# Edge scores of two graph attention layers as products of two rows per graph, in strips of the TensorE array

## The chip, the cores and the metric

The kernel runs on one core of a Trainium2 chip. Its time is the device time of one execution in microseconds (us), the median of several runs.

The kernel treats 128 graphs in 32 groups of four, and in the steady part every group takes the same time. In the trace I take the distance from the first `pw` matmul of one group to that of the next, and call the median the **period**.

## The reference

Two layers on `x` [128 graphs, 128 nodes, 256] with an adjacency matrix for each graph. The first is a relational attention with eight heads and a feed-forward network (FFN). The second, which the change touches, has two graph attention layers, then a norm, an FFN and another norm:

```
def _gat(h, adj, W, a, out_features):
    Wh  = h @ W
    Wh1 = Wh @ a[:out_features]          # one number per node
    Wh2 = Wh @ a[out_features:]          # one number per node
    e = leaky_relu(Wh1 + swapaxes(Wh2, 1, 2), 0.2)     # 128 x 128 edge scores
    att = softmax(where(adj > 0, e, -9e15), axis=1)
    return att @ Wh
h = _gat(x, adj, W1, a1); h = _gat(h, adj, W2, a2)
h = layernorm(residual + h); out = layernorm(h + ffn(h))
```

The edge scores of a graph are an outer sum of two vectors.

## The kernel before

All matmuls are fp32. The order of TensorE is written by hand: `beside(main, side)` puts units of an FFN between the pieces of the graph layers, and a `yield n` in a piece means "n FFN units here". A unit is two `ph` matmuls of 128x512 with one ScalarE activation (`hT`), or four `po` matmuls of 128x256; either occupies TensorE for about 1.72 us. The matmuls write to eight buffers in the memory called PSUM: four `ps_s`, two `ps_av` ("av" and "den"), two `ps_mm` for the FFN.

The outer sum was made of a broadcast and a bias. `pb` has the one vector in all 128 rows (a matmul whose stationary operand is one column repeated 128 times), and ScalarE adds the other vector as a bias for each partition:

```
def edges(pb, bias, S, l):
    for b in range(G):                                          # G = 4 graphs
        nc.scalar.activation(s[:, b, :], pb[:, b*P:(b+1)*P], AF.Identity, bias=bias(b))
    nc.vector.scalar_tensor_tensor(s, s, ALPHA, s, op0=ALU.mult, op1=ALU.max)   # leaky relu
    nc.scalar.activation(s, s, AF.Exp)
    ...                                  # mask, row sums, reciprocal; POOL multiplies

def layer1(S, after):
    ...
    yield 4
    yT = transposed(...)                       # pt -> yT
    yield 1
    for b in range(G):                         # pw -> wh, in ps_s
        ...
    pb = ps_av.tile([P, T], F32, tag="den")
    for c in range(NCH):                       # NCH = 2, T = 512
        nc.tensor.matmul(pb, wb[:, c, :], yT[:, c, :], ...)
    att = edges(pb, lambda b: wh[:, b, D+2:D+3], S, 0)
    after()                                    # transposes of the next group: pt, in ps_s
    yield 5
    for b in range(G):
        nc.tensor.matmul(py[:, :D+1], att[:, b, :], wh[:, b, :D+1], ...)
        nc.scalar.copy(yh[:, b, :], py[:, :D+1])
        nc.tensor.matmul(pb[:, b*P:(b+1)*P], wh[:, b, D+1:D+2].to_broadcast([P, P]), att[:, b, :], ...)
    att = edges(pb, lambda b: yh[:, b, D:D+1], S, 1)
    yield 5
    ...                                        # pg: att @ yh
```

## Time and profile before

| quantity | before |
|---|---|
| time, median | 3167.5 us |
| period of a group | 95.48 us |
| TensorE busy | 95% of the span |
| TensorE waits for `hT`, second FFN (beside the graph layers) | 25.9 us in all |
| TensorE waits for `hT`, first FFN | 34.3 us in all |

The page and the timelines that carry the argument are shown in the prediction. One view more: the list of who waited for whom, TensorE's part (us in total, times, the longest). Three lines are shown; those left out come once or twice each, the largest a wait of 37.1 us for weights at the start.

```profile
PE ph L279 <- ACT hT L283: 60.2, 60, 1.1
PE pt L259 <- DVE t L242: 16.1, 5, 6.5
PE py L466 <- POOL gs L436: 6.5, 1, 6.5
```

Only the first line recurs in each group: twice, once in the FFN beside the graph layers and once in the other FFN. The other two belong to the ends of the kernel, where there is no FFN to fill the time.

### The profile page before, as it was taken

The page shows a single profiled execution, that of the slowest core. Times are in us where ns is not written, and L with a number is a line of the kernel's source. Part 1 is how long each engine was busy: PE and PEld are TensorE (multiplying, and loading weights), DVE is VectorE, ACT ScalarE, POOL GpSimd, SP SyncE. Part 2 cuts the span into 40 slices and gives each one's busy share as a digit, 9 for nine tenths or more (in the row PEclk, how much of TensorE's full clock was granted, in tenths as well). Part 3 has the DMA queues.
Part 4 walks back from the last instruction along what each step waited for, and adds up shares of the span by engine and source line. Part 5 has one row for each costly group of instructions (what it writes and reads, how often), then busy time and mean ns, then how long its engine had stood idle before and what let it go on. Part 6 is the DMA issues. An engine that isn't in the chain of part 4 may idle for free.

```text
span 3165.2 us, 42834 instructions
## 1 busy us (share of the span) xinstructions
PE 3015.7 (95%) x18062; PEld 2016.9 (64%) x18062; DVE 1636.4 (52%) x3433; ACT 1139.4 (36%) x1958; POOL 747.4 (24%) x360
## 2 busy tenths in 40 slices
PE   4899999999999999999999999999999999999997
PEld 2556667666666666666666666666666666676664
DVE  3544465554465554565554555544555644555622
ACT  1333333434333334333334333334333334334332
POOL 0212221212222212222212222212212212212222
PEclk9999999999999999999999999999999999999998
DMA  4000000000000000000000000000000000000000
GB/s 148 21 17 17 24 18 17 21 24 18 18 23 18 21 24 18 17 18 24 21 18 24 17 17 21 24 18 24 17 17 21 24 18 24 18 17 8 8 7 14
DMA packets 58101, 69.80 MB, mean 22 GB/s; under 512 B 6704, under 2 KB 44720, under 8 KB 57904
## 3 DMA queue, kind: packets, MB, share of 16 engines
q1 hardware_dynamic: 51632, 64.76, 6.7%
q10 hardware_dynamic: 6272, 2.25, 0.4%
q8 instruction: 144, 2.36, 0.3%
q14 instruction: 53, 0.43, 0.0%
HBM read 50.22 MB, written 16.78 MB: 21 GB/s over the span
## 4 chain that ended last, share of the span: by engine, by line
PE 88%; ACT 9%; DVE 1%; DMA 1%; issue 0%; POOL 0%; ACTq 0%; SPq 0%; POOLq 0%; DVEq 0%
PE po L290 28%; PE ph L279 23%; PE pv L391 7%; PE pq L381 5%; PE pav L351 4%; PE pw L451 4%; PE pwo L411 3%; PE ps L318 2%; PE pt L259 2%; PE pden L341 2%; PE py L466 2%; PE pg L481 2%; PE pb L458 2%; ACT yT L262 1%; ACT L426 1%; ACT L238 1%
## 5 line engine op out<-in xcount | busy, mean ns | idle before, releaser
L279 PE MATMUL ph<-yT,w_L_gnn_W 128*128 128x512 f32 x1024 | 484.9, 597 | 34.3 <-ACT hT L283 34.3
L279 PE MATMUL ph<-yT,w_L_gnn_w_ff 128*128 128x512 f32 x1024 | 464.5, 597 | 25.9 <-ACT hT L283 25.9
L249 POOL TENSOR_TENSOR res<-t,r_L_gnn_g 128x1024 f32<-128x1024 f32 x64 | 150.7, 2355 | 1375.4 <-DVE rs L240 1335.6
L290 PE MATMUL po<-w_L_gnn_W,hT 128*128 128x256 f32 x2048 | 472.1, 384 | 0.0
L290 PE MATMUL po<-w_L_gnn_w_ff,hT 128*128 128x256 f32 x2048 | 457.5, 379 | 0.0
L242 DVE TENSOR_SCALAR t<-t,mv,rs 128x256 f32<-128x256 f32 x384 | 447.6, 1226 | 3.5
L290 PEld LDWEIGHTS po<-w_L_gnn_w_ff,hT 128*128 128x128 f32 x2048 | 386.5, 190 | 65.3 <-issue 14.8
L290 PEld LDWEIGHTS po<-w_L_gnn_W,hT 128*128 128x128 f32 x2048 | 381.4, 190 | 62.2 <-issue 6.6
L279 PEld LDWEIGHTS ph<-yT,w_L_gnn_W 128*128 128x128 f32 x1024 | 192.8, 191 | 290.2 <-issue 223.4
L395 DVE TENSOR_TENSOR v<-pv,r_L_gnn_bv 128x512 f32<-128x512 f32 x128 | 88.6, 692 | 489.5 <-PE pv L391 489.5
L279 PEld LDWEIGHTS ph<-yT,w_L_gnn_w_ff 128*128 128x128 f32 x1024 | 187.8, 191 | 239.6 <-issue 178.7
L283 ACT ACTIVATE hT<-ph,c_L_gnn_b 128x512 f32<-128x512 f32 x256 | 175.9, 688 | 452.7 <-PE ph L279 452.4
L249 POOL TENSOR_TENSOR res<-t,r_L_gnn_g_ln 128x1024 f32<-128x1024 f32 x64 | 150.4, 2350 | 453.2 <-DVE rs L240 388.7
L391 PE MATMUL pv<-wv,xT 128*128 128x512 f32 x512 | 240.2, 592 | 0.0
L283 ACT ACTIVATE hT<-ph,c_L_gnn_b_ff 128x512 f32<-128x512 f32 x256 | 171.7, 682 | 162.5 <-PE ph L279 162.5
L358 DVE RECIPROCAL rd<-pden 128x512 f32<-128x512 f32 x64 | 214.3, 3349 | 20.4 <-PE pden L341 20.3
L326 DVE TENSOR_TENSOR pm<-e,adj 128x512 f32<-128x512 f32 x256 | 159.5, 684 | 114.7 <-ACT e L325 114.7
L238 ACT ACTIVATE sd<-mv,eps 128x4 f32<-128x4 f32 x96 | 28.1, 292 | 501.1 <-DVE mv L236 501.1
L235 DVE BATCH_NORM_STATS2 st<-t 128x6 f32<-128x256 f32 x512 | 192.7, 413 | 6.6
L325 ACT ACTIVATE e<-ps 128x512 f32<-128x512 f32 x256 | 132.2, 602 | 151.6 <-PE ps L318 151.3
L436 POOL TENSOR_TENSOR gs<-gs,gr 128x512 f32<-128x512 f32 x64 | 66.6, 1041 | 496.9 <-DVE gr L435 484.8
L391 PEld LDWEIGHTS pv<-wv,xT 128*128 128x128 f32 x512 | 94.9, 190 | 108.1 <-issue 108.1
(101 smaller groups left out, 3705.9 us busy)
## 6 DMA issues: line engine op xcount, KB each, us to landing
xT<-in_xT_dram SPq DMA_DIRECT2D x32, 512.0 KB, 3.7
x<-in_x_dram SPq DMA_DIRECT2D x32, 512.0 KB, 3.9
out_dram<-res SPq DMA_DIRECT2D x32, 512.0 KB, 2.9
adj<-in_adjT_dram SPq DMA_DIRECT2D x32, 256.0 KB, 2.7
w_L_gnn_W<-in_L_gnn_W_dram SPq DMA_DIRECT2D x2, 1024.0 KB, 8.2
w_L_gnn_w_ff<-in_L_gnn_w_ff_dram SPq DMA_DIRECT2D x2, 1024.0 KB, 12.1
wv<-in_L_gnn_Wv_dram SPq DMA_DIRECT2D x2, 256.0 KB, 7.0
temp<-in_L_gnn_a_dram ACTq DMA_DIRECT2D x2, 256.0 KB, 9.8
```

The costliest lines, as they stand in the source:

```text
L235: nc.vector.bn_stats(st[:, b, :], t[:, b, :])
L242: nc.vector.tensor_scalar(t[:, b, :], t[:, b, :], mv[:, b, 0:1], rs[:, b : b + 1], op0=ALU.subtract, op1=ALU.mult,)
L249: nc.gpsimd.tensor_mul(o, y, over(gr))
L279: nc.tensor.matmul(ph, wa[:, c, f * P : (f + 1) * P], inT[:, c, :], start=(c == 0), stop=(c == NCH - 1),)
L283: nc.scalar.activation(hT[:, f, :], ph, func, bias=ba[:, f : f + 1])
L290: nc.tensor.matmul(po[:, s * D : (s + 1) * D], hT[:, f, b * P : (b + 1) * P], wb_[:, f, :], start=(f == 0), stop=(f == NF - 1),)
L325: nc.scalar.activation(e[:, s], pss[s], AF.Exp, scale=SCALE)
L326: nc.vector.tensor_mul(pm[:, s], e[:, s], ad[:, 2 * p : 2 * p + 2, None, :].to_broadcast([P, 2, NCH, P]),)
L351: nc.tensor.matmul(pav[s * DH : (s + 1) * DH, u, c, :], v[:, d0 : d0 + DH], m[:, s, u, c, :], start=(r == 0), stop=(r == 1),)
L358: nc.vector.reciprocal(rd, pden)
L381: nc.tensor.matmul(pq, w[:, c, m * P : (m + 1) * P], xt[:, c, :], start=(c == 0), stop=(c == NCH - 1),)
L391: nc.tensor.matmul(pv, xt[:, c, b * P : (b + 1) * P], wv[:, c].rearrange("p r d -> p (r d)"), start=(c == 0), stop=(c == NCH - 1),)
```

## The change

The intent is to make TensorE's part cheaper. An outer sum is a product of two pairs of rows: (u, 1) against (1, v). `ends` makes the two rows of each graph as matmuls with 32 stationary columns, one graph in each 32-column strip of the array. `edges` multiplies them as matmuls over 32 rows, one graph in each 32-row strip. Four such matmuls are meant to run side by side. The diff is abridged.

```diff
+    def ends(lhs, rhs, n):
+        pr = ps_av.tile([P, P], F32, tag="den", name="pr_" + n)
+        for c in range(len(lhs)):
+            for b in range(G):
+                nc.tensor.matmul(pr[b * DH : (b + 1) * DH, :], lhs[c](b), rhs[c](b), ...)
+        src = ...; tgt = ...
+        nc.vector.tensor_scalar(src, pr, rows01[:, 1:2], rows01[:, 0:1], op0=ALU.mult, op1=ALU.add)
+        nc.scalar.activation(tgt, pr, AF.Identity, bias=rows01[:, 1:2], scale=rows01[:, 0:1])
+        return src, tgt
-    def edges(pb, bias, S, l):
+    def edges(src, tgt, S, l):
-        for b in range(G):
-            nc.scalar.activation(s[:, b, :], pb[:, b*P:(b+1)*P], AF.Identity, bias=bias(b))
-        nc.vector.scalar_tensor_tensor(s, s, ALPHA, s, op0=ALU.mult, op1=ALU.max)
+        pes = [ps_s.tile([P, T], F32, tag="s", ...) for b in range(G)]
+        for b in range(G):
+            rows = slice(b * DH, (b + 1) * DH)
+            nc.tensor.matmul(pes[b][:, :P], src[rows, :], tgt[rows, :], start=True, stop=True)
+        for b in range(G):
+            pe = pes[b][:, :P]
+            nc.scalar.activation(s[:, b, :], pe, AF.Copy, scale=ALPHA)
+            nc.vector.tensor_max(s[:, b, :], pe, s[:, b, :])
...
         yield 1
+        both = ends(..., n + "_0")                # ahead of pw
...                                                # pw -> wh
-        pb = ...; matmul(pb, wb, yT)
-        att = edges(pb, ..., S, 0)
+        yield 1
+        att = edges(*both, S, 0)
         after()
-        yield 5
+        yield 4
+        both = ends([lambda b: wh[:, b, :DH]], [lambda b: att[:, b, :]], n + "_1")
...                                                # py; the second pb is gone
-        att = edges(pb, ..., S, 1)
-        yield 5
+        yield 1
+        att = edges(*both, S, 1)
+        yield 4
```

The weights prepared at the start change to match (`wr` in place of `wb`, two columns fewer beside the products). The number of FFN units stays the same; one of each five moves ahead of `edges`.

More of the change, by code (lines that the diff above doesn't have):

```diff
@@ L174, in mm_tile @@
         return ps_mm.tile([P, T], F32, tag="mm", name=name)
-    NU = D + 3
+    NU = D + 2
     temp = flat(w1p.tile([P, NF, T], F32, tag="hT", name="temp"))
@@ L193, in fast_pass @@
     wa2 = k.columns(gw2, a2, scr, "2")
-    rhs = cut(NCH, D + 2)
-    nc.vector.tensor_copy(rhs[:, :, :D], gw2)
-    nc.vector.tensor_copy(rhs[:, :, D : D + 1], wa2[:, :, 1:2])
-    nc.vector.tensor_copy(rhs[:, :, D + 1 : D + 2], wa2[:, :, 0:1])
+    rhs = cut(NCH, NU)
+    nc.vector.tensor_copy(rhs[:, :, :2], wa2)
+    nc.vector.tensor_copy(rhs[:, :, 2:], gw2)
     gw1T = cut(NCH, D)
@@ L206, in fast_pass @@
     wu = k.tile([P, NCH, NU], "wu")
-    wb = k.tile([P, NCH, P], "wb")
+    wr = k.tile([P, NCH, DH], "wr")
+    nc.vector.memset(wr, 0.0)
+    nc.vector.tensor_copy(wr[:, :, :2], wa1)
     for m in range(NCH):
@@ L211, in fast_pass @@
             nc.tensor.matmul(
-                pu[:, : D + 2], gw1T[:, c, m * P : (m + 1) * P], rhs[:, c, :],
+                pu[:, :NU], gw1T[:, c, m * P : (m + 1) * P], rhs[:, c, :],
                 start=(c == 0), stop=(c == NCH - 1),
             )
-        nc.scalar.copy(wu[:, m, : D + 2], pu[:, : D + 2])
-        nc.vector.tensor_copy(wu[:, m, D + 2 :], wa1[:, m, 1:2])
-        nc.vector.tensor_copy(wb[:, m, :], wa1[:, m, 0:1].to_broadcast([P, P]))
+        nc.scalar.copy(wu[:, m, :], pu[:, :NU])
+    rows01 = k.tile([P, 2], "rows01")
+    strips = k.ident.rearrange("p (s r) -> p r s", r=DH)
+    nc.vector.tensor_reduce(rows01, strips[:, 0:2, :], AX.X, ALU.add)
     c_adj = k.tile([P, NG], "c_adj")
@@ L415, in layer0 @@
             added(t, p, po, xr)
-    def edges(pb, bias, S, l):
+    def ends(lhs, rhs, n):
+        pr = ps_av.tile([P, P], F32, tag="den", name="pr_" + n)
+        for c in range(len(lhs)):
+            for b in range(G):
+                nc.tensor.matmul(
+                    pr[b * DH : (b + 1) * DH, :], lhs[c](b), rhs[c](b),
+                    start=(c == 0), stop=(c == len(lhs) - 1),
+                )
+        src = w1p.tile([P, P], F32, tag="src", name="src_" + n)
+        tgt = w1p.tile([P, P], F32, tag="tgt", name="tgt_" + n)
+        nc.vector.tensor_scalar(
+            src, pr, rows01[:, 1:2], rows01[:, 0:1], op0=ALU.mult, op1=ALU.add
+        )
+        nc.scalar.activation(
+            tgt, pr, AF.Identity, bias=rows01[:, 1:2], scale=rows01[:, 0:1]
+        )
+        return src, tgt
+    def edges(src, tgt, S, l):
         n = f"{S['g']}_{l}"
         s = w2p.tile([P, G, P], F32, tag="gs", name="gs_" + n)
+        pes = [ps_s.tile([P, T], F32, tag="s", name=f"pe_{n}_{b}") for b in range(G)]
         for b in range(G):
-            nc.scalar.activation(
-                s[:, b, :], pb[:, b * P : (b + 1) * P], AF.Identity, bias=bias(b)
-            )
-        nc.vector.scalar_tensor_tensor(s, s, ALPHA, s, op0=ALU.mult, op1=ALU.max)
+            rows = slice(b * DH, (b + 1) * DH)
[4 more added lines that the diff above has]
+            nc.vector.tensor_max(s[:, b, :], pe, s[:, b, :])
         nc.scalar.activation(s, s, AF.Exp)
@@ L446, in layer1 @@
         yield 1
+        both = ends(
+            [lambda b, c=c: wr[:, c, :] for c in range(NCH)],
+            [lambda b, c=c: yT[:, c, b * P : (b + 1) * P] for c in range(NCH)], n + "_0",
+        )
         wh = w1p.tile([P, G, NU], F32, tag="wh", name="wh_" + n)
@@ L455, in layer1 @@
             nc.scalar.copy(wh[:, b, :], pw[:, :NU])
-        pb = ps_av.tile([P, T], F32, tag="den", name="pb_" + n)
-        for c in range(NCH):
-            nc.tensor.matmul(pb, wb[:, c, :], yT[:, c, :], start=(c == 0), stop=(c == NCH - 1))
-        att = edges(pb, lambda b: wh[:, b, D + 2 : D + 3], S, 0)
+        yield 1
+        att = edges(*both, S, 0)
         after()
-        yield 5
-        yh = w1p.tile([P, G, D + 1], F32, tag="yh", name="yh_" + n)
-        pb = ps_av.tile([P, T], F32, tag="av", name="pb2_" + n)
+        yield 4
+        both = ends([lambda b: wh[:, b, :DH]], [lambda b: att[:, b, :]], n + "_1")
+        yh = w1p.tile([P, G, D], F32, tag="yh", name="yh_" + n)
         for b in range(G):
             py = ps_s.tile([P, T], F32, tag="s", name=f"py_{n}_{b}")
-            nc.tensor.matmul(
-                py[:, : D + 1], att[:, b, :], wh[:, b, : D + 1], start=True, stop=True
-            )
-            nc.scalar.copy(yh[:, b, :], py[:, : D + 1])
-            nc.tensor.matmul(
-                pb[:, b * P : (b + 1) * P], wh[:, b, D + 1 : D + 2].to_broadcast([P, P]),
-                att[:, b, :], start=True, stop=True,
-            )
-        att = edges(pb, lambda b: yh[:, b, D : D + 1], S, 1)
-        yield 5
+            nc.tensor.matmul(py[:, :D], att[:, b, :], wh[:, b, 2:], start=True, stop=True)
+            nc.scalar.copy(yh[:, b, :], py[:, :D])
+        yield 1
+        att = edges(*both, S, 1)
+        yield 4
         S["t2"] = t = w3p.tile([P, G, D], F32, tag="t", name="t2_" + n)
@@ L481, in layer1 @@
                 nc.tensor.matmul(
-                    po[:, s * D : (s + 1) * D], att[:, b, :], yh[:, b, :D], start=True, stop=True
+                    po[:, s * D : (s + 1) * D], att[:, b, :], yh[:, b, :], start=True, stop=True
                 )
```

## The prediction

> **What bounds the kernel now.** I read the page first, for the busiest engine and the chain that ended last, then the groups of the lines that the change removes, then the timeline of TensorE and of ScalarE through one period of the loop (32 groups of four graphs; a period is about 98 us). The page:
>
> ```profile
> PE 3015.7 (95%) x18062; PEld 2016.9 (64%) x18062; DVE 1636.4 (52%) x3433; ACT 1139.4 (36%) x1958; POOL 747.4 (24%) x360
> PE 88%; ACT 9%; DVE 1%; DMA 1%; issue 0%; POOL 0%; ACTq 0%; SPq 0%; POOLq 0%; DVEq 0%
> ```
>
> TensorE is busy for 95% of the span and is 88% of the chain. Its program order is fixed by hand, so the time is the sum of what its instructions occupy plus the waits inside that order. VectorE (52%) and ScalarE (36%) matter only where TensorE waits for them. The groups that are to go:
>
> ```profile
> L458 PE MATMUL pb<-yT,wb 128*128 128x512 f32 x128 | 60.1, 591 | 0.0
> L470 PE MATMUL pb<-gs,wh 128*128 128x128 f32 x256 | 50.1, 278 | 0.0
> ```
>
> They have 110 us of busy time together, but these rows overlap their neighbours. What an instruction occupies is the distance from its start to the next start, so I take that from the timeline:
>
> ```profile
> 1537.24 1.88 PE L279 MATMUL ph<-yT,w_L_gnn_W 128*128 128x512 f32 x4
> 1539.05 1.17 PE L318 MATMUL ps<-qT,kT 32*128 32x128 f32 x32
> 1540.15 3.72 PE L290 MATMUL po<-w_L_gnn_W,hT 128*128 128x256 f32 x16
> 1543.80 1.08 PE L341 MATMUL pden<-e,ones 128*32 128x128 f32 x32
> 1544.70 0.40 PE L351 MATMUL pav<-e,v 128*32 128x128 f32 x8
> 1544.92 0.40 PE L351 MATMUL pav<-pm,v 128*32 128x128 f32 x8
> ...
> 1574.13 3.67 PE L451 MATMUL pw<-wu,yT 128*128 128x259 f32 x16
> 1577.64 1.88 PE L458 MATMUL pb<-yT,wb 128*128 128x512 f32 x4
> 1579.36 1.04 PE L259 MATMUL pt<-ident,t 128*128 128x128 f32 x8
> 1580.23 3.60 PE L279 MATMUL ph<-yT,w_L_gnn_w_ff 128*128 128x512 f32 x8
> 1584.69 1.98 PE L279 MATMUL ph<-yT,w_L_gnn_w_ff 128*128 128x512 f32 x4 [0.86 <-ACT hT L283]
> 1586.51 3.62 PE L290 MATMUL po<-w_L_gnn_w_ff,hT 128*128 128x256 f32 x16
> 1589.97 0.60 PE L466 MATMUL py<-wh,gs 128*128 128x257 f32 x2
> 1590.40 0.39 PE L470 MATMUL pb<-gs,wh 128*128 128x128 f32 x2
> 1590.62 0.60 PE L466 MATMUL py<-wh,gs 128*128 128x257 f32 x2
> ```
>
> Each matmul is two records. The reader is to see four things. The first layer's pb occupies 1577.64 to 1579.36, 1.72 us. A second-layer pb occupies 0.22 us (1590.40 to 1590.62). Blocks in strips (ps, pden, pav) exist already, so the prices of the new ones can be read off. And there is one wait of TensorE in the graph layers, of 0.86 us, behind ScalarE, whose queue then is:
>
> ```profile
> 1579.64 1.14 ACT L422 ACTIVATE gs<-pb,wh 128x128 f32<-128x128 f32 x4 [1.43 <-PE pt L259]
> 1580.66 1.47 ACT L262 ACTIVATE yT<-pt,c_L_gnn_beta,c_L_gnn_g 128x512 f32<-128x512 f32 x2
> 1582.14 1.28 ACT L426 ACT_TABLE_LOAD   x1
> 1583.97 1.25 ACT L283 ACTIVATE hT<-ph,c_L_gnn_b_ff 128x512 f32<-128x512 f32 x2
> ```
>
> The third ph needs the buffer that the first of these hT empties, and that hT stands behind the edge scores, both yT, a table load and the exp.
>
> **What the Trainium skill says.** "TensorEngine Tiling (Array Packing)", Key Properties: changing the tiling mode drains TensorE. The trace agrees; the price is worked out below at 0.32 to 0.41 us for one block. "TensorE: Matmul & The Clock Gate", Part 3, says that small matmuls in different strips of the array run side by side. It agrees: four matmuls of pav (eight records) take 0.22 us, as much as one 128x128 matmul of L470. The tiling page, PSUM Bottleneck, warns that the copy out of PSUM may become the limit after such a speedup. Before, no wait of that kind shows; I expect one. "PSUM — Partial Sum Buffer", Engine vs sequencer instructions, calls the ScalarE and VectorE queues strict FIFO; the hT above, held behind the yT and the exp, agrees.
>
> **The change part by part, per group.**
> Removed from TensorE: 1.72 us (first pb) and four times 0.22 = 0.88 us (second pb), 2.60 us; over 32 groups 83 us, 2.6% of the time. The columns trimmed from pw and py are worth nothing (259 against 258).
>
> Added: four blocks in strips, `ends` and `edges` in each layer. A set of four matmuls in four strips costs 0.22 us. The switch cost: ph before ps takes 1.72 us at its usual pitch, so ps could have started at 1538.96 and started at 1539.05: entry 0.09. The ps block of four sets lasts 1540.15 - 1539.05 = 1.10, which is 0.22 more than 4 x 0.22. The po after it merges to 3.72 where an undisturbed one has 3.62: 0.10. So a row-strip block costs 0.41 over its sets. For column strips pden has 0.90 - 0.88 = 0.02 inside; from the individual records of pav I get 0.09 more at the exit; with entry and the slow successor 0.32 in all. Then:
> - ends, layer 1: two chunks, 2 x 0.22 + 0.32 = 0.76 us
> - ends, layer 2: 0.22 + 0.32 = 0.54
> - edges, twice: 0.22 + 0.41 = 0.63 each, 1.26
>
> Sum 2.56 us. Against 2.60 removed, the array gains about 0.04 us per group, 1 us in the whole kernel. Four matmuls side by side are cheap, but each block is so short that the switch costs more than its work.
>
> Waits. In the first layer `edges` fills all four ps_s buffers and the transposes of the next group (pt) come straight after it; they take the buffers of graphs 0 and 1. In the kernel before, these had been emptied by then. Now each needs a ScalarE copy (0.37 us, L422's size) and after it a VectorE maximum (L361 takes 0.41 for 256 columns out of PSUM, L269 0.68 for 512, so I extrapolate 0.28 for 128). The order of ScalarE in the changed kernel puts the hT of the preceding FFN unit ahead of the copies. Let U be the end of that unit. hT starts at U + 0.21 (as the hT after other ph) and lets go after 0.6; copy of graph 0 to U + 1.18; maximum to U + 1.50; pt at about U + 1.55. Unhindered it would start at U + 0.63: a stall of 0.92 us. Graph 1's buffer follows in time for the second pt.
>
> In return the old ph wait goes: one FFN unit has moved ahead of `edges`, so after the transposes only two ph remain, whose two buffers are free. It cost 0.86 us idle, 1.03 by distance of starts (1455 ns against 429 between the records). But po then needs the buffer of the first of those ph. ScalarE has copies to U + 1.95, yT, table load, exp, yT, and hT until about U + 6.13; po would come at 1.55 + 0.87 + 2 x 1.72 = U + 5.86. I put 0.3 us there. Balance of waits: 0.92 + 0.3 - 1.03 = +0.19 us.
>
> The attention itself: its POOL multiply ended 3.3 us before py and 3.2 before the next layer's product in the kernel before (1586.66 against 1589.97). One unit of 1.72 us now lies before `edges`, so the slack falls to 1 to 2 us and stays positive. src and tgt have pw and a unit (5 us) or py and a unit (3.4 us) to be made in. VectorE gets 64 more tensor_scalar and 256 maxima instead of 64 of 0.70 us, about 40 us more of work at 52% busy; ScalarE 64 more of 0.37. Both stay off the path but for the stall above. The setup changes by less than 1 us.
>
> Sum: (-0.04 + 0.19) x 31 = about 5 us more, 3172 us.
>
> **The rivals.**
> (1) The intended gain. If the switches were hidden (weights loaded ahead of the drain), five sets of 0.22 us, 1.1 us, would replace 2.60: -48 us, 3119 us, 1.5% faster. With the copies hidden too and the ph wait gone as well, 32 us more, 3087. For it: the array does less work, and the ph wait is real. Against: all 62 po blocks after ps start alike late, and the blocks here are far shorter than ps.
> (2) The copies cost more. If ScalarE or VectorE is behind when `edges` ends, or a maximum takes 0.5 us, the stall is 1.5 to 2 us: +20 to +35 us, 3190 to 3205. For it: two engines in series on a FIFO. Against: VectorE is idle in that stretch of the timeline before.
> (3) The attention arrives late. If the shortened slack is used up, each layer waits 1 us: +60 us, 3230. For it: slack falls by half or more. Against: the second layer's copies and maxima overlap, where before the maximum waited for all four.
>
> **Range and chances.** The terms nearly cancel, and each is uncertain by some tenths of a us per group; 0.5 us per group is 16 us. From (1) half true to (2): 3150 to 3205. Over 2% faster needs below 3104, only (1) with the waits gone too: 0.04. Over 2% slower needs above 3231, (3) together with (2): 0.04. Within 2%: 0.92.
>
> **What would show it.** Right: the distance from start to start over the four new blocks is near 2.5 us per group; pt shows a wait of some 0.9 us behind VectorE's maximum, 31 times, about 30 us in all; the ph wait of the second FFN (25.9 us in all) is gone and a shorter one stands at po; py and pg wait for no attention. Wrong: new blocks near 1.1 us (then rival 1), a pt wait over 1.5 us (rival 2), a wait for POOL's multiply at `ends`, py or pg (rival 3).

## The result, and the profile after

| quantity | before | after |
|---|---|---|
| time, median | 3167.48 us (4 runs) | 3169.39 us (4 runs) |
| ratio to before, 95% interval | | 1.0006, 0.9989 to 1.0023 |
| period of a group | 95.48 us | 95.61 us |

A ratio is the mean time of the one kernel's fast runs over the mean of the other's in the same rounds, so it isn't quite the ratio of the medians. The forecast was 3172 us, within 2% with a chance of 0.92. The two kernels can't be told apart by their times, but by their periods they can: 0.13 us more per group.

The page of the changed kernel, engines and chain:

```profile
PE 3012.4 (95%) x18958; PEld 1988.7 (63%) x18958; DVE 1665.2 (53%) x3687; ACT 1135.2 (36%) x2022; POOL 747.5 (24%) x360
PE 87%; ACT 9%; DVE 2%; DMA 1%; issue 1%; POOL 0%; SPq 0%; POOLq 0%; DVEq 0%; ACTq 0%
```

The reader is to see that nothing has changed on this level: TensorE has 896 records more and is as busy as before. VectorE's share of the chain went from 1 to 2%. Now the groups that replace the two `pb`, and the FFN group whose wait was to go (busy us, mean ns; idle before, and what ended it):

```profile
L282 PE MATMUL ph<-yT,w_L_gnn_w_ff 128*128 128x512 f32 x1024 | 461.4, 594 | 0.0
L447 PE MATMUL pe<-tgt,src 32*128 32x128 f32 x512 | 33.5, 321 | 0.8 <-ACT wh L485 0.8
L426 PE MATMUL pr<-yT,wr 128*32 128x128 f32 x512 | 21.3, 283 | 0.2 <-ACT yT L265 0.2
L426 PE MATMUL pr<-gs,wh 128*32 128x128 f32 x256 | 13.9, 289 | 4.9 <-POOL gs L462 4.9
```

By busy time the change looks like a gain: 110.2 us of `pb` gave way to 68.7 us. The row of the FFN beside the graph layers has lost its 25.9 us of idle time. Yet the total is the same. The waits of TensorE show one part of the reason (three lines of the list):

```profile
PE ph L282 <- ACT hT L286: 35.4, 31, 1.8
PE pt L262 <- DVE gs L451: 25.2, 30, 0.8
PE po L293 <- ACT hT L286: 5.6, 30, 0.2
```

A wait of 25.2 us at the transposes, behind VectorE's maximum, and one of 5.6 us at `po` stand where 25.9 us stood before. The other part is in the timeline, where distances from start to start are read. This is TensorE in one group after the change:

```profile
1572.84 1.88 PE L282 MATMUL ph<-yT,w_L_gnn_w_ff 128*128 128x512 f32 x4
1574.65 0.65 PE L426 MATMUL pr<-yT,wr 128*32 128x128 f32 x16
1575.23 3.75 PE L481 MATMUL pw<-wu,yT 128*128 128x258 f32 x16
1578.82 1.88 PE L282 MATMUL ph<-yT,w_L_gnn_w_ff 128*128 128x512 f32 x4
1580.63 0.50 PE L447 MATMUL pe<-tgt,src 32*128 32x128 f32 x8
1581.97 1.09 PE L262 MATMUL pt<-ident,t 128*128 128x128 f32 x8 [0.84 <-DVE gs L451]
1582.90 3.60 PE L282 MATMUL ph<-yT,w_L_gnn_w_ff 128*128 128x512 f32 x8
1586.68 3.72 PE L293 MATMUL po<-w_L_gnn_w_ff,hT 128*128 128x256 f32 x16 [0.19 <-ACT hT L286]
1590.34 0.43 PE L426 MATMUL pr<-gs,wh 128*32 128x128 f32 x8
1590.69 1.99 PE L494 MATMUL py<-wh,gs 128*128 128x256 f32 x8
1592.52 1.89 PE L293 MATMUL po<-w_L_gnn_w_ff,hT 128*128 128x256 f32 x8
1594.34 0.50 PE L447 MATMUL pe<-tgt,src 32*128 32x128 f32 x8
1594.78 7.17 PE L293 MATMUL po<-w_L_gnn_w_ff,hT 128*128 128x256 f32 x32
```

Take the second `pe`, from 1592.52. The `po` unit before it would let it start at 1594.24 (1.72 us later); it starts at 1594.34. The block lasts until 1594.78, 0.44 us for four matmuls of which a set costs 0.22 in steady flow. The first `po` after it then takes 0.32 us to the next record where 0.22 is usual. In sum, by the single records, 0.63 us for 0.22 us of work, as the prediction had it.

The wait at `pt` has its cause on two other engines, ScalarE and VectorE in the same stretch:

```profile
1580.74 0.69 ACT L286 ACTIVATE hT<-ph,c_L_gnn_b_ff 128x512 f32<-128x512 f32 x1 [1.34 <-PE ph L282]
1581.32 0.77 ACT L450 ACTIVATE gs<-pe 128x128 f32<-128x128 f32 x4
1581.62 0.88 DVE L451 TENSOR_TENSOR gs<-pe,gs 128x128 f32<-128x128 f32 x4 [5.17 <-ACT gs L450]
```

The `hT` of the unit ahead runs first, then the four copies, and each maximum follows its copy. The buffers of graphs 0 and 1 come free through these, and `pt` begins at 1581.97, 1.43 us after the end of the unit (1578.82 + 1.72 = 1580.54).

### The profile page after: what moved, and what is told of

The parts are those of the page before. It is cut to its first block, busy times and chain, and to the rows that moved or that the text cites. A ratio compares the mean times of both kernels' runs of the same rounds, so it can differ in the third digit from the quotient of the medians.

```text
span 3167.1 us, 44877 instructions
## 1 busy us (share of the span) xinstructions
PE 3012.4 (95%) x18958; PEld 1988.7 (63%) x18958; DVE 1665.2 (53%) x3687; ACT 1135.2 (36%) x2022; POOL 747.5 (24%) x360
## 4 chain that ended last, share of the span: by engine, by line
PE 87%; ACT 9%; DVE 2%; DMA 1%; issue 1%; POOL 0%; SPq 0%; POOLq 0%; DVEq 0%; ACTq 0%
PE po L293 29%; PE ph L282 23%; PE pv L394 7%; PE pq L384 5%; PE pav L354 4%; PE pw L481 4%; PE pwo L414 4%; PE pt L262 3%; PE ps L321 2%; PE pden L344 2%; PE py L494 2%; PE pg L504 2%; ACT hT L286 2%; ACT yT L265 1%; ACT L452 1%; ACT L286 1%
## 5 line engine op out<-in xcount | busy, mean ns | idle before, releaser
L293 PE MATMUL po<-w_L_gnn_w_ff,hT 128*128 128x256 f32 x2048 | 468.9, 382 | 5.6 <-ACT hT L286 5.6
L451 DVE TENSOR_TENSOR gs<-pe,gs 128x128 f32<-128x128 f32 x256 | 56.7, 283 | 223.1 <-ACT gs L450 223.1
```

The source lines that it names most:

```text
L293: nc.tensor.matmul(po[:, s * D : (s + 1) * D], hT[:, f, b * P : (b + 1) * P], wb_[:, f, :], start=(f == 0), stop=(f == NF - 1),)
```

## The experiments

The theory has two parts: (a) in the steady order the strips cost the array as much as the matmuls that they replace, because each short block pays for two changes of the tiling mode; (b) the wait at `pt` comes from the PSUM buffers, and is as large as the ScalarE wait that went away. The rival to (a) is that strips cost by their work, so that a gain of 1.5% is there and is hidden by something. The rival to (b) is that ScalarE's queue is the limit and a wait only moves.

**Transposes one unit later, in the changed kernel.**

```diff
         att = edges(*both, S, 0)
+        yield 1
         after()
-        yield 4
+        yield 3
```

> The changed kernel with one FFN unit moved between the first layer's edges and the next group's transposes, so that the copies out of PSUM have 1.7 us before their buffers are wanted. Theory (the array gains nothing, the stall at the transposes is real and nothing stands behind it): the 25 us wait for the VectorE maximum goes, and the small wait at po (5.6 us) with it; 26 to 34 us less than the changed kernel, 3135 to 3143 us, ratio to before 0.990 to 0.993. Rival (ScalarE's queue is the real limit, the stall only moves to the next ph or po): 3160 to 3170 us, with a new wait of 0.5 us or more per group for hT.

Measured: 3133.66 us, ratio 0.9891 (0.9876 to 0.9906); period 94.30 us, 1.31 us under the changed kernel. That is 1.3 us below the range expected: the gain was a little larger. The timeline of TensorE has no wait in this stretch any more:

```profile
1564.18 0.50 PE L447 MATMUL pe<-tgt,src 32*128 32x128 f32 x8
1564.62 1.99 PE L282 MATMUL ph<-yT,w_L_gnn_w_ff 128*128 128x512 f32 x4
1566.44 1.04 PE L262 MATMUL pt<-ident,t 128*128 128x128 f32 x8
1567.31 1.88 PE L282 MATMUL ph<-yT,w_L_gnn_w_ff 128*128 128x512 f32 x4
1569.03 3.62 PE L293 MATMUL po<-w_L_gnn_w_ff,hT 128*128 128x256 f32 x16
```

Between `pe` and `pt` stands now a `ph` unit, 1.82 us in which the copies and maxima finish. The wait at `po` went too, since ScalarE has the `hT` of that unit ahead of both `yT`. By distances from start to start in both traces, from `pe` to the next record gave back 0.91 us (1.34 against 0.43), and the same matmuls from there to the next `pr` 0.40 (8.36 against 7.96): together the 1.31 of the period. So both waits were real and nothing stood behind them: part (b) holds and its rival falls.

**The same move in the kernel before.**

```diff
         att = edges(pb, lambda b: wh[:, b, D + 2 : D + 3], S, 0)
-        after()
-        yield 5
+        yield 1
+        after()
+        yield 4
```

> The kernel before with the same move of one unit, nothing else. Theory: its own wait (ph for hT, 25.9 us idle, 1.03 us per group between starts) goes, 26 to 33 us less: 3134 to 3141 us, as fast as the changed kernel with the move, so that the strips themselves are worth less than 5 us. Rival (the move helps only the strips): 3160 to 3170 us, and the changed kernel with the move is 25 us ahead of this one.

Measured: 3149.88 us, ratio 0.9944 (0.9931 to 0.9958); period 94.95 us. This was a miss: half of the gain expected. The wait at `ph` is gone, but a smaller one has come at `po` (TensorE, then ScalarE):

```profile
1573.85 1.04 PE L259 MATMUL pt<-ident,t 128*128 128x128 f32 x8
1574.72 3.60 PE L279 MATMUL ph<-yT,w_L_gnn_w_ff 128*128 128x512 f32 x8
1578.64 3.72 PE L290 MATMUL po<-w_L_gnn_w_ff,hT 128*128 128x256 f32 x16 [0.33 <-ACT hT L283]
```

```profile
1576.58 1.43 ACT L262 ACTIVATE yT<-pt,c_L_gnn_beta,c_L_gnn_g 128x512 f32<-128x512 f32 x2
1577.91 1.26 ACT L283 ACTIVATE hT<-ph,c_L_gnn_b_ff 128x512 f32<-128x512 f32 x2
```

`po` needs the buffer that the first of these `hT` empties. That `hT` stands behind both `yT` on ScalarE and begins at 1577.91, although its `ph` was done about 1.5 us before (the two `ph` units begin at 1574.72, so the first ends near 1576.44). Here the rival to (b) was right for the kernel before: the wait moved. Taken alone, this run would have said that the strips are worth 16 us.

**Two units in the kernel before.** The edit is the same with `yield 2`, `after()`, `yield 3`, so that this `hT` comes ahead of the `yT`.

> The kernel before with two FFN units, not one, ahead of the transposes. The first move left 0.49 us per group at po, because hT of the unit after the transposes stood behind both yT on ScalarE. Theory: with two units that hT is ahead of them, the wait is gone, and the kernel before loses the other 15 us: 3132 to 3139 us, level with the changed kernel with its move (3133.7), so that the strips are worth nothing for the array. Rival (the strips' own chain is shorter for ScalarE and that is a lasting gain): it stays near 3150 us.

Measured: 3133.29 us, ratio 0.9895 (0.9880 to 0.9910); period 94.35 us. No wait recurs in the graph layers, and the kernel before is level with the changed kernel and its move (3133.66 us, period 94.30):

```profile
1563.08 3.60 PE L279 MATMUL ph<-yT,w_L_gnn_w_ff 128*128 128x512 f32 x8
1566.52 1.04 PE L259 MATMUL pt<-ident,t 128*128 128x128 f32 x8
1567.39 1.88 PE L279 MATMUL ph<-yT,w_L_gnn_w_ff 128*128 128x512 f32 x4
1569.11 3.62 PE L290 MATMUL po<-w_L_gnn_w_ff,hT 128*128 128x256 f32 x16
```

With the waits gone on both sides, the strips are worth 0.05 us per group. The prediction's account of the array said 0.04. This settles part (a) for both layers together.

**Strips in the first layer only.** The second layer gets back its full-array `pb` and its bias (abridged; the columns of `wh` and `yh` change to match):

```diff
-        both = ends([lambda b: wh[:, b, :DH]], [lambda b: att[:, b, :]], n + "_1")
...
+            nc.tensor.matmul(
+                pb[:, b * P : (b + 1) * P], wh[:, b, 0:1].to_broadcast([P, P]),
+                att[:, b, :], start=True, stop=True,
+            )
-        att = edges(*both, S, 1)
+        att = edges_sum(pb, lambda b: yh[:, b, 0:1], S, 1)       # the old edges
```

> Changed kernel with the second graph layer as it was before. Theory: in the second layer the strips add 0.54 + 0.63 us and remove 0.88, so that undoing them there saves about 0.29 us per group: 9 us under the changed kernel, about 3160 us (3155 to 3165). Rival (strips cost by their work, 0.44 us for the 0.88 removed): undoing them costs 14 us, about 3183 us.

Measured: 3163.94 us, ratio 0.9989 (0.9975 to 1.0003); period 95.33 us, 0.29 us under the changed kernel. The median lies 5.5 us under it rather than 9, within the noise of the runs; the period agrees with the expectation to 0.01 us.

**Strips in the second layer only.** The first layer gets back `wb`, `pb` and its order (`after()` right after the old edges, then `yield 5`); the second keeps `ends` and `edges`.

> The other half: strips in the second layer alone, the first layer and its order as before. Theory: 0.29 us per group more than before, 9 us: about 3176 us (3172 to 3181), and the ph wait of 25.9 us is still there. Rival (strips cost by their work): 14 us less, about 3153 us.

Measured: 3176.22 us, ratio 1.0025 (1.0011 to 1.0039); period 95.76 us, 0.28 us over the kernel before. The wait list has the old `ph` wait of both FFNs back:

```profile
PE ph L282 <- ACT hT L286: 61.4, 61, 1.8
```

Both halves agree: in the second layer the strips lose 0.28 to 0.29 us per group. The rival, cost by work, had both signs the other way.

**The price of a switch by itself.** Two more sets of four strip matmuls, whose results nobody reads, added to the changed kernel. First joined to the first layer's `ends`, in the same mode:

```diff
+    def extra(yT, n):
+        px = ps_av.tile([P, P], F32, tag="av", name="px_" + n)
+        for b in range(G):
+            nc.tensor.matmul(px[b * DH : (b + 1) * DH, :], wr[:, 0, :], yT[:, 0, b * P : (b + 1) * P], ...)
...
+        extra(yT, n + "_a"); extra(yT, n + "_b")       # right after ends
```

> The changed kernel with two more sets of four strip matmuls per group, whose results nobody reads, appended to the first layer's ends, in the same tiling mode. Theory: each set costs its work alone, 0.22 us: 2 x 0.22 x 32 = 14 us, about 3183 us (3180 to 3188).

Measured: 3194.04 us, ratio 1.0086 (1.0073 to 1.0100); period 96.34 us, 0.73 us more where 0.44 was expected. In the trace's single records the second set starts 360 ns after the last burst of the first, where 89 ns is usual, while the first set follows `pr` at 89 ns. The second set took a new tile in the only buffer of "av". The list of waits names the cause (PEld is the loading of weights):

```profile
PEld px_b L443 <- PE px_a L443: 11.5, 32, 0.5
```

The first record of the second set waits for a semaphore that the last matmul of the first set raises: TensorE waits for its own earlier write to that buffer, once in each group. The mended run takes this wait away.

**The joined sets, mended**, both in different columns of one tile:

```diff
-        px = ps_av.tile([P, P], F32, tag="av", name="px_" + n)
+        px = ps_av.tile([P, 2, P], F32, tag="av", name="px_" + n)
```

> The joined sets again, mended: in the first try the second set took a new tile in the buffer of the first, and TensorE waited 0.27 us for its own write (360 ns between the records against 89). Now both sets write different columns of one tile. Theory: 2 x 0.22 x 32 = 14 us over the changed kernel (3169.4): 3183 us (3180 to 3187), and the distance from the first pr record to the first pw record grows from 0.574 to 1.01 us. Rival (a set costs 0.39 us even when joined, as the first try read): 3194 us.

Measured: 3184.98 us, ratio 1.0054 (1.0041 to 1.0068); period 96.04 us, 0.43 us more for two sets. TensorE:

```profile
1583.56 0.65 PE L426 MATMUL pr<-yT,wr 128*32 128x128 f32 x16
1584.02 0.62 PE L444 MATMUL px<-yT,wr 128*32 128x128 f32 x16
1584.57 3.75 PE L491 MATMUL pw<-wu,yT 128*128 128x258 f32 x16
```

From `pr` to `pw` 1.01 us, where the changed kernel has 0.58 (1574.65 to 1575.23). The second set now follows the first at 89 ns. So a set in the mode already set costs 0.22 us.

**The same two sets apart**, each between two `po` units:

```diff
         after()
-        yield 4
+        yield 3
+        extra(yT, n + "_a")
+        yield 1
...
         att = edges(*both, S, 1)
-        yield 4
+        yield 2
+        extra(yT, n + "_b")
+        yield 2
```

> The same two sets, but each by itself between matmuls of the whole array (between two po units). Theory: each costs 0.22 + 0.32 us of switching: 2 x 0.54 x 32 = 35 us, about 3204 us (3199 to 3210), 21 us over the joined ones. Rival (a strip block costs its work and the switch is hidden): the same 14 us as joined, about 3183 us.

Measured: 3207.8 us, ratio 1.0131 (1.0115 to 1.0146); period 96.71 us, 1.10 us more for two sets, 0.55 us each. (The profiled execution, 3201.16 us, was the fastest of the four. The medians would give 38.4 us, or 0.60 each.) TensorE around the first:

```profile
1600.79 1.99 PE L293 MATMUL po<-w_L_gnn_w_ff,hT 128*128 128x256 f32 x8 [0.18 <-ACT hT L286]
1602.71 0.43 PE L443 MATMUL px_a<-yT,wr 128*32 128x128 f32 x8
1603.07 1.99 PE L293 MATMUL po<-w_L_gnn_w_ff,hT 128*128 128x256 f32 x8
```

The same work costs 0.22 us joined and 0.55 apart. The difference, 0.33 us, is the way into the column-strip mode and out of it; the prediction had 0.32. That shows part (a) directly for column strips. For row strips it rests on the 0.63 us of the second `pe` and on the two runs with strips in one layer.

What TensorE does in that time is not separated by these runs. The weight loads around the same block show one thing:

```profile
1602.71 0.16 PEld L443 LDWEIGHTS px_a<-yT,wr 128*32 128x32 f32 x8 [0.33 <-issue]
1603.06 0.51 PEld L293 LDWEIGHTS po<-w_L_gnn_w_ff,hT 128*128 128x128 f32 x3 [0.20 <-issue]
```

Within the stream of `po` a load starts about 0.22 us ahead of its matmul (1602.19 for the one at 1602.40, by the single records). At both edges of the block it starts together with its matmul (1602.71, and 1603.06 for 1603.07). That a short matmul with weights of its own costs this by itself is ruled out by the kernel before: there each `pb` of the second layer, 128 columns of the whole array between two `py`, took 0.22 us, and the `py` after it 0.44, twice 0.22.

**What paid of both.** Strips in the first layer alone, with the transposes one unit later (two of the edits above together).

> Strips in the first layer alone, with the transposes one unit later: what paid of both. Theory: the changed kernel with the move (3133.7) less the 5 us that undoing the second layer's strips brought: 3128 us (3124 to 3132), ratio to before about 0.9875. Rival (the two gains overlap): 3133 us.

Measured: 3122.73 us, ratio 0.9860 (0.9845 to 0.9875); period 94.02 us, 0.28 us under the changed kernel with the move. This is the fastest of all, 1.4% under the kernel before, and 1.3 us below the range expected. The loss of the second layer shows here a third time (0.28 us). Against the kernel before with two units, also free of recurring waits (94.35), the strips of the first layer gain 0.33 us per group, which is what the prediction's terms give for it (1.72 - 0.76 - 0.63). Most of the gain is the order: 1.13 us of the 1.47 us per group came to the kernel before by moving two units.

The periods side by side, in us:

| kernel | period | against |
|---|---|---|
| before | 95.48 | |
| changed | 95.61 | +0.13 before |
| changed, second layer as before | 95.33 | -0.29 changed |
| before, second layer in strips | 95.76 | +0.28 before |
| changed, transposes one unit later | 94.30 | -1.31 changed |
| before, one unit later | 94.95 | -0.54 before |
| before, two units later | 94.35 | -1.13 before |
| first layer in strips, one unit later | 94.02 | -1.47 before |
| changed, two more sets joined (mended) | 96.04 | +0.43 changed |
| changed, two more sets apart | 96.71 | +1.10 changed |

## Why the prediction was right

It said 3172 us; 3169.39 us was measured. The nearly equal terms did cancel as it said, and each was found where it was put. That the balance fits to 0.02 us per group is partly luck, since two terms of the waits missed by about 0.1 us in opposite directions, as shown below. The prediction's period of about 98 us is 95.48 in the trace; nothing was worked out from it.

- **The four blocks.** Forecast 0.76, 0.54 and twice 0.63 us per group. By the single records of the trace (entry, block, slow successor) the first `ends` took 0.77, the second 0.55 and the second `edges` 0.63 us; the first `edges` can't be measured here, as the stall covers its exit, but takes 0.63 in the run with the transposes later. The strips' gain on the array with all waits gone is 0.05 us per group; forecast 0.04.
- **The stall at the transposes.** Forecast `pt` at U + 1.55 us, U being the end of the unit ahead; it came at U + 1.43, since a copy took 283 ns on the mean where 370 had been put. But the time without a stall, U + 0.63, was as much too late: it counted the slow successor, which is `pt` itself, and by the single records the block ends at U + 0.53. So the delay is 0.91 us where 0.92 was forecast. The idle time of 25.2 us in 30 waits was forecast as about 30 in 31. The buffers were shown to be the cause by the move of one unit.
- **The old wait.** It went from 25.9 us to none in the second FFN, as forecast. Its worth was put at 1.03 us per group; taking it away alone, with two units in the kernel before, gave 1.13. The 0.10 left out is the slow first `ph` after the wait.
- **The new wait at `po`.** Forecast 0.3 us; the profile has 0.19 us of idle time in each group. By starts, `pt` to `po` is 4.71 us (1581.97 to 1586.68) where 0.87 + 2 x 1.72 = 4.31 would do, so 0.4 us are lost there, 0.06 of it in `pt` itself: 0.1 more than forecast.
- **The balance.** Forecast +0.15 us per group; the period has +0.13. The runs give the split: the moves took 1.31 us from the changed kernel and 1.13 from the one before, so the waits were 0.18 worse (forecast 0.19), and behind the moves the strips gain 0.05. Over 31 groups that is 4 us; the medians differ by 1.9 us, and the interval of the ratio has room for both.
- **The attention's slack.** Forecast to fall from 3.3 to 1 to 2 us and to stay positive. The multiply on POOL ended 2.35 us before the second `ends` and 1.69 before `pg` (medians over the groups of the trace): enough, the first a bit more than forecast.
- **VectorE and ScalarE.** VectorE's busy time rose by 28.8 us rather than 40 and ScalarE's fell by 4 us where 24 more were forecast. VectorE's 256 maxima have a mean of 283 ns but 56.7 us in all, not 72: they overlap, and adding single durations counts this twice. ScalarE's 256 copies were shorter as well as overlapping: 283 ns and 50.2 us in all, where the 256 with a bias had 368 ns and 73.2 us. Neither was on the path but for the stall.

The rival of the intended gain fell with the sets apart. Rival (2), dearer copies, fell with the measured 1.43 us. Rival (3), late attention, shows in no wait that recurs. What the prediction didn't see is that the kernel before had nearly as much to gain from its order as the changed one (1.13 against 1.31 us per group): the wait at `ph` was taken as given there, and it took two units to remove it.

## What to carry to other kernels

Before splitting a small matmul into strips of the array, count the blocks, not the work: here a set of four cost 0.22 us and a block of its own 0.3 to 0.4 us more, so strips pay only where they replace long matmuls (1.72 us in the first layer, a gain of 0.33) or can stand together with other strip work. Read the gain off distances from start to start; the busy times of the groups promised 41 us that were not there. When work is moved into shared buffers, look at who takes those buffers next: here moving one unit of other work in between was worth 1.1%, ten times what the strips moved. And give the old kernel the same help before crediting the new one.

## What the Trainium skill lacked or had wrong

- "TensorEngine Tiling (Array Packing)", Key Properties, says that a change of mode drains TensorE but gives no price. Here a block of column strips between full-array matmuls cost 0.33 us over its work (0.55 against 0.22 us), and a block of row strips 0.41 us (0.63 against 0.22, by the single records around the second `pe`).
- "TensorE: Matmul & The Clock Gate", Part 3, Measured speedup vs the span model, puts the starts of matmuls in different strips about 4 ns apart. In the single records, fp32, they are 6 to 7 ns apart within a burst of four, and bursts follow each other at 89 ns.
- No page that I read says what it costs when TensorE waits for a semaphore of its own last matmul, as it did here for a reused buffer. In the first run with joined sets the gap was 360 ns instead of 89; with one tile for both sets the period shrank by 0.30 us.
